# Attention and FFN block on one core: all eight row tiles of a sample in four pairs, and the work around them moved

## The chip, the cores and the metric

The kernel runs on one core of a Trainium2 chip. The time is the device time of one execution in microseconds (us). A core has five engines with queues of their own, and each queue is worked off in order: TensorE (PE in the profile; its weight loads are PEld), VectorE (DVE), ScalarE (ACT), GpSimd (POOL), and SyncE (SP), which issues most of the DMAs.

## The reference

For each of 8 samples `x` has 1024 rows and 256 columns. What is computed, cut to what matters:

```
mod = (silu(c) @ wmod).reshape(8, 6, 1, 256)          # sa, ca, ga, sb, cb, gb; |ga|, |gb| at least 0.25
h = layernorm(x) * (1 + ca) + sa
scores = (h * w_lhs) @ (h * w_rhs).T                  # 1024 x 1024 for each sample
x = x + ga * (softmax(scores) @ h)
h = layernorm(x) * (1 + cb) + sb
x = x + gb * (relu(h @ W1 + b1) @ W2 + b2)            # 256 -> 1024 -> 256
```

All in float32.

## The kernel before, in words

**Tiles.** A sample `b` has eight row tiles `i` of 128 rows. The main loop runs over samples and, in each, over eight steps, one for each tile. Step `i` issues the scores of tile `i + 2` (`direct`), which are copied from PSUM to SBUF by ScalarE (L419). Scores are symmetric (both sides are the same rows, weighted by w_lhs times w_rhs), so only the upper part is computed; the rest comes by a transpose on VectorE (`mirror`, L435) and five DMAs through DRAM (`move`, four writes and one read). VectorE takes the row maximum (L463), TensorE turns it into a row (`max_turn`, L468), VectorE subtracts it (`subtract`, L475), ScalarE takes the exponent (L484). The result is `pT`, the transposed weights of tile `i`: eight blocks of 128x128.

**Product with the values.** `xg` holds the values, eight blocks of 128 rows with 256 columns and a column of ones, whose product is the softmax's sum. A single tile takes eight products 257 columns wide (`product`, L501, tile `po`), a division and a residual addition on VectorE (`product_out`, L513, L515), and the statistics for the next layernorm (L241, L242). A pair of tiles (`i`, `i + 1`) is seen as a 2x2 block product and takes seven half-size products in place of eight: four products of half the rows and 128 or 129 columns are one of the seven. `pair_begin` does two of the seven (L549, tile `pp`), ScalarE copies one of them to `W` (L555), VectorE adds (`pair_begin_sum`, L561). `pair_end` does the other five (L593, tiles `pq` and `pr`), and `pair_out` adds up, divides and adds the residual on VectorE (L608 to L621). The five need sums of the two tiles' weights: `s1` (L565), and three that overwrite parts of `pT` (L575 to L577), all on POOL (`left_sum`, `left_sums`). They also need sums of the values, `tsum`, once for each sample, on POOL too (`right_sums`, L534).

**FFN.** The FFN of the rows of the sample before (its first four tiles in steps 0 to 3, its last four in steps 4 to 7) runs in between. The hidden layer is made in four chunks `c`, two in each of the steps 0 and 1 (4 and 5): `pair_products` (L726; `pa`, `pb`, `pc`), a copy `kept` of `pa` by ScalarE (L747), sums on VectorE (L762 to L771), one more product into `pa` (in `pair_last`, it waits for `kept`), its sum on VectorE (L779), a sum on POOL (L780), the relu on ScalarE (L789, L790), and four sums on POOL (`pair_turn`, L799 to L802, tile `ft`) for the second layer. The second layer is `y_first` in steps 2 and 6 and `y_second` in steps 3 and 7 (L806; `ya` to `yd`), with sums on VectorE (L828 to L830, L848 to L851). Then `y_gate` (ScalarE, L857), `y_turn` (transposes on VectorE, L867, and DMAs) and `y_add` (POOL, L880) bring y back to rows, and `y_out` writes them.

**Order.** All is written out by hand: at the end every instruction is pinned to the order in which it was issued on its engine. `spare` takes one operation from a queue of POOL operations that have no fixed place (`later`). PSUM tiles `pa`, `pb`, `pc`, `pp`, `po`, `pq`, `pr`, `ya` to `yd` share four buffers, so that a product also waits for the reader of an older tile. `Y` has one buffer.

Before the change the tiles of a sample are taken as: 0 alone, 1 and 2, 3 and 4, 5 alone, 6 and 7. In step 0 and 5 stands `product`; pair 1 begins in step 1 and ends in step 2; pair 3 begins in step 3 and ends in step 4; pair 6 begins in step 6 and ends in step 7. The part that decides on it, in the loop's step:

```
if i in (0, 5):
    product(b, i)
    product_out(b, i)
elif i == 1:
    pair_begin(b, i)
    pair_begin_sum(b, i)
elif i == 3:
    left_sums(b, i)
elif i in (2, 4) or i == NT - 1 and ahead:
    pair_end(b, i - 1)
    pair_out(b, i - 1)
```

The first sample (b = 0) has a loop body of its own, with single products only; the change doesn't touch it. After the last sample its FFN follows alone.

Of the kernel before, what the change touches and what calls it, by code (L numbers as in the profile page):

```python
# [11 lines left out]
F32 = mybir.dt.float32  # L12
AF = mybir.ActivationFunctionType
ALU = mybir.AluOpType
# [10 lines left out]
def adaln_block_kernel(  # L25
# [534 lines left out]
        rows = slice(P, P + XS)  # L560
        nc.vector.tensor_tensor(W[:, 0, rows], pp[:, XS : 2 * XS], W[:, 1, rows], ALU.add)  # L561

    def left_sum(b, i):
        s1 = two_t["s1"] = work.tile([P, TH, P], F32, tag="s1", name=f"s1_{b}_{i}", bufs=1)
        nc.gpsimd.tensor_tensor(s1, *halves(pT_t[b, i + 1]), ALU.add)  # L565

    def left_sums(b, i):


        if "s1" not in two_t:  # L570
            left_sum(b, i)
        (a11, a12), (a21, a22) = halves(pT_t[b, i]), halves(pT_t[b, i + 1])
        s1 = two_t["s1"]
        add = nc.gpsimd.tensor_tensor
        add(a21, a11, a21, ALU.subtract)  # L575
        add(a11, s1, a11, ALU.subtract)
        add(a12, a12, a11, ALU.subtract)  # L577
# [66 lines left out]
    def ffn_rstd(b, g):  # L644
        mv = mvb_t.pop((b, g))
        ffn["r", g] = mv, rstd_of(mv, "rb", f"rb_{b}_{g}")
# [206 lines left out]
    def y_gate(b):  # L853

        Y = ffn["Y"]
        for h in range(2):
            nc.scalar.activation(  # L857
                Y[:, h], Y[:, h], AF.Identity,
                scale=gcol[:, 0, h, b : b + 1], bias=gcol[:, 1, h, b : b + 1],
            )  # L860

    def y_turn(b, g, hurry=False):

        Y = ffn["Y"]
        T = two.tile([P, NV, NT * V], F32, tag="T", name=f"T_y{b}_{g}", bufs=3)
        for h in range(2):
            nc.vector.transpose(  # L867
                T.rearrange("p a (t h u) -> p a t h u", h=2, u=V)[:, :, :, h, :],
                Y[:, h].rearrange("p (t a v) -> p a t v", a=NV, v=V),
            )  # L870
        Y = Y.rearrange("p h r -> p (h r)").rearrange("p (b m) -> p b m", b=NV)
        move(Y, T, NT * V, f"y{b}_{g}", hurry)
        ffn["rows", b, g] = Y.rearrange("p b (t h u) -> p t h b u", h=2, u=V)
# [276 lines left out]
    for b in range(B):  # L1150
        for i in range(NT):
# [63 lines left out]
            if first:  # L1215

                ub, ug = (b - 1, 0) if i >= TH else (b - 2, 1)
                back = i % TH == 0 and ub >= 0
                pair_products(fb, fg, c, turn_max)
                if i == 0:  # L1220
                    ffn_rstd(b - 1, 1)
                if i == 4:
                    y_gate(fb)
                    if b + 1 < B:
                        prepare_rstd(b + 1, 1)
                if i == TH + 1:
                    pair_relu(c - 1)
                pair_sums(fb, fg, c)
                if (b, i) == (1, 0):
                    subtract(*late)  # L1230
                if i == 4:
                    y_turn(fb, 0)
                if ahead:
                    mirror(*ahead)
                pair_last(fb, fg, c)
                if i == 0 and back:
                    for q in range(2):
                        y_add(ub, ug, q)
                if i == TH + 1:
                    pair_turn(c - 1)  # L1240
                if late and i != 4 and (b, i) != (1, 0):
                    subtract(*late)
                pair_products(fb, fg, c + 1, (lambda: max_turn(*extra)) if extra else None)
                if (b, i) == (1, 0):
                    exponent(*late)
                    late = None
                if (b, i) == (B - 1, 5):
                    ffn_rstd(b, 0)
                if i == 5:
                    exponent(*late)  # L1250
                    if b + 1 < B:
                        prepare_turn_apart(b + 1, 1, 1)
                        prepare_turn_apart(b + 1, 1, 0)
                if i == 1:
                    exponent(*late)
                    left_sum(b, i)
                elif i == 4 and b + 1 < B:
                    prepare_norm(b + 1, 1)
                    x_plus(b + 1, 1)
                pair_relu(c)  # L1260
                sides_too = i == 4 and b + 1 < B
                if sides_too:
                    prepare_turn_apart(b + 1, 0, 1)
                if late and i == 0:
                    exponent(*late)
                if sides_too:
                    prepare_turn_apart(b + 1, 0, 0)
                middle(b, i)
                pair_sums(fb, fg, c + 1)
                pair_last(fb, fg, c + 1)  # L1270
                if i == 4:
                    if b + 1 < B:
                        prepare_blocks(b + 1, 1)
                        xg_times(b + 1, 1)
                    weights(*late)
                if ahead and ahead != extra:
                    row_max(*ahead)
                pair_turn(c)
                if i == 0:
                    pair_relu(c + 1)  # L1280
                    pair_turn(c + 1)
                if i == 4:
                    for q in range(2):
                        y_add(ub, ug, q)
                if c > 0:
                    pair_relu(c + 1)
                    pair_turn(c + 1)
            else:
                half = i % TH - 2
                if i == NT - 2:  # L1290
                    for q in (1, 3):
                        if (b, q) in two_t:
                            pair_stats(b, q)
                if i == 2:
                    left_sums(b, 1)
                elif i == 3:
                    pair_begin(b, i, turn_max)
                elif i == 6:
                    pair_begin(b, i, lambda: (max_turn(*late), weights(*late)))
                elif not ahead:  # L1300

                    pair_end(b, i - 1)
                    pair_out(b, i - 1)
                    pair_stats(b, i - 1)
                if half:
                    y_second(fb, fg, turn_max if i == NT - 1 else None)
                else:
                    y_first(fb, fg, turn_max if i == 2 else None)
                if ahead:
                    mirror(*ahead)  # L1310
                if i == 2 and b + 1 < B:
                    prepare_rstd(b + 1, 0)
                elif i == 6 and b + 1 < B:
                    ffn_rstd(b, 0)
                elif i == NT - 1 and b == B - 1:
                    ffn_rstd(b, 1)
                if i in (3, 6):
                    pair_begin_sum(b, i)
                if i == 2:
                    weights(*late)  # L1320
                elif i == 6:
                    left_sums(b, i)
                spare()
                early(b, i)
                if late and half:
                    weights(*late)
                middle(b, i)
                if i == 2 and b + 1 < B:
                    load_x(b + 1, 1)
                spare()  # L1330
                if ahead:
                    row_max(*ahead)
                if half:
                    y_second_sums(fb)
                    if i == NT - 1:
                        y_gate(fb)
                    elif b + 1 < B:
                        prepare_stats(b + 1, 1)
                else:
                    y_first_sums()  # L1340
                spare()
            if extra:
                subtract(*extra)
            if i == NT - 1 and 0 < b < B - 1:
                y_turn(fb, fg, True)
            turns(b, i)
            norms(b, i)
            if extra:
# [1 line left out]
            if not first:  # L1350
                for _ in range(4 if half else 1):
                    spare()
            if i in (0, 5):
                product(b, i)
                product_out(b, i)
            elif i == 1:
                pair_begin(b, i)
                pair_begin_sum(b, i)
            elif i == 3:
                left_sums(b, i)  # L1360
            elif i in (2, 4) or i == NT - 1 and ahead:
                pair_end(b, i - 1)
                pair_out(b, i - 1)
                if i == NT - 1:
                    assert not queue
                    right_sums(b + 1, range(4))
                if i == NT - 1 or b == B - 1:
                    pair_stats(b, i - 1)
            late = ahead if ahead != extra else None
            if first and back:  # L1370
                y_out(ub, ug)
            if i == 0 and b + 1 < B:
                load_rows(b + 1)
# [78 lines left out]
```

## Time and profile before

| | |
|---|---|
| median of 3 runs | 756.9 us (756.22 to 757.13) |
| the profiled execution | 756.93 us, span 755.1 us |
| granted TensorE clock | 1.000 |
| busy: TensorE, VectorE, POOL, ScalarE | 749.1, 574.9, 570.9, 374.9 us |
| from one sample's scores of tile 2 to the next one's (b = 4 to 5) | 90.43 us (343.70 to 434.13) |

Times in the profile's rows are microseconds from the start of the span. A row of the timeline gives start, length, engine, line, operation, the tile written and those read, the shape, and how many were merged; in square brackets the engine's idle time before it and what ended it. A float32 product shows as two instructions, so that a count of x8 is four products. Products overlap in their pipeline: what one costs is read from the starts of two that follow each other. In the windows view each engine has its busy time and count of instructions.

### The profile page before, as it was taken

How to read it: one execution, taken by the hardware profiler on the slowest of the kernel's cores; microseconds unless marked ns; L12 is line 12 of the kernel's file. 1: busy time of each engine (PE TensorE's matmuls, PEld its weight loads, DVE VectorE, ACT ScalarE, POOL GpSimd, SP SyncE). 2: the span in 40 equal slices, each digit the busy share in tenths (PEclk: the TensorE clock that was granted, in tenths of full speed). 3: DMA queues.
4: the chain of work that ended last, by engine and by line, in shares of the span. 5: the costliest groups of instructions: out<-in, count | busy, mean ns of one | idle time of the engine just before them, and what ended most of it. 6: DMA issues, size and time to landing. Idle time of an engine off the chain costs nothing.

```text
span 755.1 us, 11883 instructions
## 1 busy us (share of the span) xinstructions
PE 749.1 (99%) x3876; PEld 623.4 (83%) x3876; DVE 574.9 (76%) x1259; ACT 374.9 (50%) x688; POOL 570.9 (76%) x658
## 2 busy tenths in 40 slices
PE   8999999999999999999999999999999999999998
PEld 4686889788897888888888878988889788888887
DVE  7787879778796879968878688876889777685632
ACT  4554646635375454745546444563546535252521
POOL 3762796878968798788877699777996888669741
PEclk9999999999999999999999999999999999999999
DMA  9033442455443453445534555245553354133220
GB/s 308 16 112 98 131 133 74 135 178 152 127 120 123 153 153 110 147 118 158 164 99 119 153 154 161 74 127 172 155 152 85 119 166 133 50 91 126 84 85 28
DMA packets 106213, 95.21 MB, mean 126 GB/s; under 512 B 29700, under 2 KB 98848, under 8 KB 106152
## 3 DMA queue, kind: packets, MB, share of 16 engines
q1 hardware_dynamic: 98408, 85.81, 38.6%
q10 hardware_dynamic: 7744, 8.65, 3.7%
q8 instruction: 30, 0.49, 0.3%
q14 instruction: 31, 0.25, 0.1%
HBM read 50.62 MB, written 43.81 MB: 125 GB/s over the span
## 4 chain that ended last, share of the span: by engine, by line
PE 96%; DMA 1%; DVE 1%; ACT 1%; issue 0%
PE psc L412 16%; PE pa L726 11%; PE po L501 10%; PE pr L593 7%; PE pb L726 7%; PE pc L726 7%; PE yc L806 6%; PE ya L806 6%; PE yb L806 6%; PE pq L593 5%; PE pp L549 5%; PE py L916 4%; PE yd L806 3%; DMA wm<-in_L_wmod_dram 1%; PE pm L468 1%; PE pmr L194 0%
## 5 line engine op out<-in xcount | busy, mean ns | idle before, releaser
L412 PE MATMUL psc<-rT,lT 128*128 128x512 f32 (+3 forms) x384 | 134.8, 487 | 0.0
L780 POOL TENSOR_TENSOR f<-f,kept 128x512 f32<-128x512 f32 x64 | 81.5, 1274 | 42.8 <-DVE f L779 20.1
L419 ACT COPY sc<-psc 128x512 f32<-128x512 f32 (+3 forms) x96 | 44.7, 476 | 119.9 <-PE psc L412 113.0
L484 ACT ACTIVATE pT<-pT 128x1024 f32<-128x1024 f32 x64 | 67.6, 1056 | 70.6 <-DVE pT L475 70.5
L475 DVE TENSOR_TENSOR pT<-sc,pm 128x1024 f32<-128x1024 f32 x64 | 77.3, 1208 | 29.3 <-PE pm L468 13.7
L412 PEld LDWEIGHTS psc<-rT,lT 128*128 128x128 f32 x384 | 66.4, 191 | 37.2 <-issue 25.6
L501 PE MATMUL po<-xg,pT 128*128 128x257 f32 x352 | 80.6, 380 | 0.0
L463 DVE TENSOR_REDUCE m<-sc 128x1 f32<-128x1024 f32 x64 | 77.4, 1209 | 2.2 <-ACT sc L419 1.8
L501 PEld LDWEIGHTS po<-xg,pT 128*128 128x128 f32 x352 | 66.2, 190 | 10.0 <-issue 0.7
L747 ACT COPY kept<-pa 128x512 f32<-128x512 f32 x64 | 37.4, 584 | 69.3 <-PE pa L726 69.1
L726 PE MATMUL pb<-hs,w1s 128*128 128x256 f32 x256 | 65.9, 380 | 0.1
L726 PE MATMUL pc<-hT,w 128*128 128x256 f32 x256 | 65.7, 379 | 0.0
L880 POOL TENSOR_TENSOR x<-x,Y 128x512 f32<-128x512 f32 x28 | 35.1, 1276 | 29.3 <-DMA Y<-D_y 29.3
L789 ACT ACTIVATE f<-f 128x512 f32<-128x512 f32 x64 | 39.8, 622 | 34.7 <-POOL f L780 34.7
L642 POOL TENSOR_TENSOR x<-x,rows 128x256 f32<-128x256 f32 x64 | 44.8, 732 | 13.8 <-ACT rows L1022 10.6
L726 PEld LDWEIGHTS pb<-hs,w1s 128*128 128x128 f32 x256 | 48.5, 190 | 7.3 <-DVE f L765 0.8
L726 PEld LDWEIGHTS pc<-hT,w 128*128 128x128 f32 x256 | 48.6, 190 | 6.7
L806 PE MATMUL yc<-f,w2s 128*128 128x256 f32 x224 | 51.3, 379 | 0.0
L435 DVE STREAM_TRANSPOSE Tm<-sc 128x896 f32<-128x896 f32 (+6 forms) x49 | 34.3, 701 | 20.3 <-ACT sc L419 19.6
L806 PEld LDWEIGHTS yc<-f,w2s 128*128 128x128 f32 x224 | 41.5, 190 | 8.1 <-issue 2.9
L549 PEld LDWEIGHTS pp<-xg,pT 128*128 128x128 f32 x336 | 41.9, 192 | 5.1 <-DVE st_b L241 1.4
L799 POOL TENSOR_TENSOR ft<-f 128x256 f32<-128x256 f32 x56 | 40.8, 729 | 6.8 <-ACT f L790 6.8
(166 smaller groups left out, 1821.1 us busy)
## 6 DMA issues: line engine op xcount, KB each, us to landing
D_f<-T_f SPq DMA_DIRECT2D x60, 128.0 KB, 2.5
X_f<-D_f SPq DMA_DIRECT2D x15, 512.0 KB, 3.7
D_a<-T_a SPq DMA_DIRECT2D x56, 128.0 KB, 2.8
D_y<-T_y SPq DMA_DIRECT2D x56, 128.0 KB, 2.9
Y<-D_y SPq DMA_DIRECT2D x14, 512.0 KB, 3.4
out_dram<-x SPq DMA_DIRECT2D x14, 512.0 KB, 4.4
X_a<-D_a SPq DMA_DIRECT2D x13, 512.0 KB, 3.4
x<-in_L_attn_x_dram ACTq DMA_DIRECT2D x12, 512.0 KB, 3.4
```

Of the source, the lines that this page charges most:

```text
L412: nc.tensor.matmul(psc[:, : hi - lo], lhsT=lT_t[b, i // TH][:, k, ts(i % TH, P)], rhs=rT_t[b, n][:, k, lo - n * HALF : HALF], start=(k == ...
L419: nc.scalar.copy(score_row(b, i)[:, lo // V : hi // V, :], psc[:, : hi - lo].rearrange("p (n v) -> p n v", v=V),)
L463: nc.vector.tensor_reduce(m, score_row(b, i), AX.XY, ALU.max)
L475: nc.vector.tensor_tensor(pT.rearrange("p j (a v) -> p j a v", v=V), score_columns(b, i), pm[:, :P].rearrange("p (j a v) -> p j a v", j=1, ...
L484: nc.scalar.activation(pT_t[b, i], pT_t[b, i], AF.Exp)
L501: nc.tensor.matmul(po[:, : D + 1], lhsT=pT[:, t, :], rhs=xg_t[b][:, t, 0 : D + 1], start=(t == 0), stop=(t == NT - 1),)
L549: nc.tensor.matmul(out, lhsT=lhs[:, t, :], rhs=xg_t[b][:, h * TH + t, P : P + XS], start=(t == 0), stop=(t == TH - 1),)
L593: nc.tensor.matmul(out, lhsT=lhs[:, t, :], rhs=rhs[:, t, :], start=(t == 0), stop=(t == TH - 1),)
L642: queue.append(lambda: nc.gpsimd.tensor_tensor(out, in0, row, op))
L726: nc.tensor.matmul(out, lhsT=lhsT, rhs=rhs, start=True, stop=True)
L780: nc.gpsimd.tensor_tensor(f[:, c::NH, hi], f[:, c::NH, hi], kept[:, None, hi].to_broadcast([P, 2, H2]), ALU.add,)
L806: nc.tensor.matmul(out, lhsT=lhs(c), rhs=rhs(c), start=(c == 0), stop=(c == NH - 1))
```

## The change

Four pairs in every sample from b = 1 on: 0 and 1, 2 and 3, 4 and 5, 6 and 7. A pair begins at the end of the steps 0 and 4 and near the start of the steps 2 and 6. It ends at the end of the steps 1 and 5, and for pair 2 and pair 6 at the start of the steps 3 and 7, ahead of `y_second`. In step 7 the additions `pair_out` of pair 6 stand ahead of the sums of `y_second`, and the right side's sums for the next sample are issued there, behind all that is left in POOL's queue. Gate and transposes of y (`y_gate`, `y_turn`) move from step 7 (and 4) into the steps 0 and 4, behind the sums of the first chunk; y's additions and the output's DMA move from the steps 0 and 4 to the steps 1 and 5. The left sums of pairs 0 and 4 stand in the steps 1 and 5, between the two chunks of these steps, and the sums `ft` of chunk 1 move behind them. Statistics of the finished tiles move to steps 3, 6 and 7 (for the last sample one of them to step 5).

The diff:

```diff
--- before.py
+++ after.py
@@ -560,17 +560,12 @@
         rows = slice(P, P + XS)
         nc.vector.tensor_tensor(W[:, 0, rows], pp[:, XS : 2 * XS], W[:, 1, rows], ALU.add)
 
-    def left_sum(b, i):
+    def left_sums(b, i):
+
+
         s1 = two_t["s1"] = work.tile([P, TH, P], F32, tag="s1", name=f"s1_{b}_{i}", bufs=1)
         nc.gpsimd.tensor_tensor(s1, *halves(pT_t[b, i + 1]), ALU.add)
-
-    def left_sums(b, i):
-
-
-        if "s1" not in two_t:
-            left_sum(b, i)
         (a11, a12), (a21, a22) = halves(pT_t[b, i]), halves(pT_t[b, i + 1])
-        s1 = two_t["s1"]
         add = nc.gpsimd.tensor_tensor
         add(a21, a11, a21, ALU.subtract)
         add(a11, s1, a11, ALU.subtract)
@@ -1216,11 +1211,13 @@
 
                 ub, ug = (b - 1, 0) if i >= TH else (b - 2, 1)
                 back = i % TH == 0 and ub >= 0
+                returned = i % TH == 1 and ub >= 0
                 pair_products(fb, fg, c, turn_max)
                 if i == 0:
                     ffn_rstd(b - 1, 1)
+                if back:
+                    y_gate(ub)
                 if i == 4:
-                    y_gate(fb)
                     if b + 1 < B:
                         prepare_rstd(b + 1, 1)
                 if i == TH + 1:
@@ -1228,16 +1225,17 @@
                 pair_sums(fb, fg, c)
                 if (b, i) == (1, 0):
                     subtract(*late)
-                if i == 4:
-                    y_turn(fb, 0)
+                if back:
+                    y_turn(ub, ug)
                 if ahead:
                     mirror(*ahead)
+                if i % TH == 1:
+                    left_sums(b, i - 1)
                 pair_last(fb, fg, c)
-                if i == 0 and back:
-                    for q in range(2):
-                        y_add(ub, ug, q)
-                if i == TH + 1:
+                if i % TH == 1:
                     pair_turn(c - 1)
+                if (b, i) == (B - 1, 5):
+                    pair_stats(b, 2)
                 if late and i != 4 and (b, i) != (1, 0):
                     subtract(*late)
                 pair_products(fb, fg, c + 1, (lambda: max_turn(*extra)) if extra else None)
@@ -1253,7 +1251,6 @@
                         prepare_turn_apart(b + 1, 1, 0)
                 if i == 1:
                     exponent(*late)
-                    left_sum(b, i)
                 elif i == 4 and b + 1 < B:
                     prepare_norm(b + 1, 1)
                     x_plus(b + 1, 1)
@@ -1275,35 +1272,34 @@
                     weights(*late)
                 if ahead and ahead != extra:
                     row_max(*ahead)
+                if returned:
+                    for q in range(2):
+                        y_add(ub, ug, q)
                 pair_turn(c)
                 if i == 0:
                     pair_relu(c + 1)
-                    pair_turn(c + 1)
-                if i == 4:
-                    for q in range(2):
-                        y_add(ub, ug, q)
                 if c > 0:
                     pair_relu(c + 1)
                     pair_turn(c + 1)
             else:
                 half = i % TH - 2
-                if i == NT - 2:
-                    for q in (1, 3):
-                        if (b, q) in two_t:
-                            pair_stats(b, q)
+                if i == NT - 2 and b < B - 1:
+                    pair_stats(b, 2)
                 if i == 2:
-                    left_sums(b, 1)
+                    pair_begin(b, i)
                 elif i == 3:
-                    pair_begin(b, i, turn_max)
+                    turn_max()
                 elif i == 6:
                     pair_begin(b, i, lambda: (max_turn(*late), weights(*late)))
-                elif not ahead:
-
+                else:
+                    turn_max()
                     pair_end(b, i - 1)
-                    pair_out(b, i - 1)
-                    pair_stats(b, i - 1)
+                    if not ahead:
+
+                        pair_out(b, i - 1)
+                        pair_stats(b, i - 1)
                 if half:
-                    y_second(fb, fg, turn_max if i == NT - 1 else None)
+                    y_second(fb, fg)
                 else:
                     y_first(fb, fg, turn_max if i == 2 else None)
                 if ahead:
@@ -1314,11 +1310,10 @@
                     ffn_rstd(b, 0)
                 elif i == NT - 1 and b == B - 1:
                     ffn_rstd(b, 1)
-                if i in (3, 6):
+                if not half:
                     pair_begin_sum(b, i)
-                if i == 2:
-                    weights(*late)
-                elif i == 6:
+                    if i == 2:
+                        weights(*late)
                     left_sums(b, i)
                 spare()
                 early(b, i)
@@ -1331,18 +1326,26 @@
                 if ahead:
                     row_max(*ahead)
                 if half:
+                    if i == NT - 1 and ahead:
+                        pair_out(b, i - 1)
                     y_second_sums(fb)
-                    if i == NT - 1:
+                    if i == NT - 1 and b == B - 1:
                         y_gate(fb)
-                    elif b + 1 < B:
-                        prepare_stats(b + 1, 1)
+                    elif i == 3:
+                        pair_stats(b, 0)
+                        if b + 1 < B:
+                            prepare_stats(b + 1, 1)
                 else:
                     y_first_sums()
+                    if i == NT - 2:
+                        pair_stats(b, 4)
                 spare()
             if extra:
                 subtract(*extra)
             if i == NT - 1 and 0 < b < B - 1:
-                y_turn(fb, fg, True)
+                while queue:
+                    spare()
+                right_sums(b + 1, range(4))
             turns(b, i)
             norms(b, i)
             if extra:
@@ -1350,24 +1353,16 @@
             if not first:
                 for _ in range(4 if half else 1):
                     spare()
-            if i in (0, 5):
-                product(b, i)
-                product_out(b, i)
-            elif i == 1:
+            if i in (0, 4):
                 pair_begin(b, i)
                 pair_begin_sum(b, i)
-            elif i == 3:
-                left_sums(b, i)
-            elif i in (2, 4) or i == NT - 1 and ahead:
+            elif i in (1, 3, 5):
                 pair_end(b, i - 1)
                 pair_out(b, i - 1)
-                if i == NT - 1:
-                    assert not queue
-                    right_sums(b + 1, range(4))
-                if i == NT - 1 or b == B - 1:
-                    pair_stats(b, i - 1)
+            elif i == NT - 1 and ahead:
+                pair_stats(b, i - 1)
             late = ahead if ahead != extra else None
-            if first and back:
+            if first and returned:
                 y_out(ub, ug)
             if i == 0 and b + 1 < B:
                 load_rows(b + 1)
```

## The prediction

> **What bounds the kernel now.** I read the page first, then the list of waits, then the timelines of one middle sample (b=4, which starts at 343.70) on each engine.
>
> ```profile
> span 755.1 us, 11883 instructions
> PE 749.1 (99%) x3876; PEld 623.4 (83%) x3876; DVE 574.9 (76%) x1259; ACT 374.9 (50%) x688; POOL 570.9 (76%) x658
> ...
> PE 96%; DMA 1%; DVE 1%; ACT 1%; issue 0%
> ```
>
> TensorE is the bound, and not only as an average: in the list of waits its longest wait inside a sample is 0.3 us. So a microsecond less on TensorE counts in full, and so does each wait that it meets. The timelines show how little early the others are. TensorE in the second half of the sample (tiles 4 to 7; it starts with the scores of tile 6 at 387.58):
>
> ```profile
> 394.17 0.59 PE L726 MATMUL pa<-hT,w1s 128*128 128x256 f32 x2
> 394.60 1.05 PE L593 MATMUL pr<-tsum,s 128*128 128x128 f32 x8
> ...
> 398.17 1.06 PE L593 MATMUL pr<-xg,pT 128*128 128x128 f32 x8
> 399.06 0.61 PE L412 MATMUL psc<-rT,lT 128*128 128x128 f32 x4
> 399.51 0.60 PE L726 MATMUL pa<-hT,w 128*128 128x256 f32 x2
> ...
> 402.21 0.60 PE L726 MATMUL pa<-hT,w1s 128*128 128x256 f32 x2
> ```
>
> The last product of FFN chunk 2 (402.21) overwrites half of `pa` and waits for ScalarE's copy `kept` of it. ScalarE:
>
> ```profile
> 393.98 2.08 ACT L281 ACTIVATE xg<-x,rs,ra 128x256 f32<-128x256 f32 x4 [0.76 <-DVE rs L277]
> 395.97 0.61 ACT L789 ACTIVATE f<-f 128x512 f32<-128x512 f32 x1
> ...
> 397.01 1.50 ACT L342 ACTIVATE rT<-X_a,sides 128x512 f32<-128x512 f32 x2
> 398.42 1.51 ACT L342 ACTIVATE lT<-X_a,sides 128x512 f32<-128x512 f32 x2
> 399.83 1.04 ACT L484 ACTIVATE pT<-pT 128x1024 f32<-128x1024 f32 x1
> 400.77 0.24 ACT L419 COPY sc<-psc 128x128 f32<-128x128 f32 x1
> 400.92 0.58 ACT L747 COPY kept<-pa 128x512 f32<-128x512 f32 x1
> ```
>
> It works without a gap from 393.98 to 401.50, and is 0.7 us early. POOL in the first half (from 343.70):
>
> ```profile
> 352.51 2.52 POOL L880 TENSOR_TENSOR x<-x,Y 128x512 f32<-128x512 f32 x2
> 354.98 1.27 POOL L780 TENSOR_TENSOR f<-f,kept 128x512 f32<-128x512 f32 x1
> ...
> 371.27 0.73 POOL L800 TENSOR_TENSOR ft<-ft,f 128x256 f32<-128x256 f32 x1
> ```
>
> Its `ft` of chunk 3 ends at 372.00; TensorE's third `ya` group (371.29, four steps of 0.43) reads it at 372.59: 0.6 us early. The windows view (busy us of TensorE, its weight loads, VectorE, ScalarE, POOL, with instructions in brackets) says the same of the stage: POOL is busy 41.3 of the first half's 43.9 us, though 76% over the whole.
>
> ```profile
> 343.70:387.60 43.90, 43.90 (x231) 36.92 (x230) 34.95 (x78) 19.75 (x38) 41.28 (x49) 1.00 0.53 153
> 387.60:434.10 46.50, 46.50 (x253) 39.52 (x252) 36.42 (x80) 27.96 (x49) 32.53 (x37) 1.00 0.42 123
> ```
>
> **The change part by part, TensorE.** Removed per sample: two single products, 3.46 us each (352.44 to 355.90). Added: one pair, 1.79 (L549, 364.22 to 366.01) + 4.46 (L593, 394.60 to 399.06) = 6.25. Gain 0.67 us, over seven samples 4.7. But the order changes too, and this is where I expect the loss. In the times below t counts from each half's first score product; where TensorE "comes" is the sum of its pieces without waits.
>
> **Second half: ScalarE comes too late.** The 4.46 us of the pair's end stood between chunks 1 and 2; now its beginning (1.79) stands there. TensorE comes to chunk 2's last product at 7.02 (394.60) + 1.79 + 0.45 + 2.70 (399.51 to 402.21) = 11.96, before 14.63. ScalarE's row up to `kept` starts from `rs` on VectorE, which follows chunk 0's products, all before the edit's place; it ends at 13.92 as before, plus one `W` copy queued ahead (L555, 0.26): 14.15. Wait 2.2 to 2.4, I take 2.3. Behind the waiting product all of chunk 3 is queued, so nothing overtakes. It holds for samples 1 to 6. The last sample has no `xg` and no `rT`/`lT` there (5 us less).
>
> **First half: y's rows and the left sums.** Gate (L857, two, 1.5 us) and transposes (L867, 1.3 us) of y move from the step before to between chunk 0's sums and its last sum L779 on VectorE. That sum ends at 8.7 instead of 7.43 (350.75 + 0.38), and chunk 1's at 12.15 instead of 10.84. `pp` of pair 0 takes the buffer that L779 frees: wait 0.2. ScalarE's relu waits for POOL's L780 behind L779, so its row (relu 1.2, exponent 1.0, `X_f` 2.1, relu 1.2, `W`, scores) brings `kept` of chunk 2 at 16.7; TensorE comes at 8.74+1.79+2.17+2.70 = 15.4, before 17.07. Wait 1.3 to 1.5.
>
> Longer still is POOL. All of pair 0's left sums, 4 x 1.27 = 5.1 (rows L565, L575 to L577), stand ahead of chunk 2 and 3, where before only one (1.27) did; the additions of y's rows (2.5) no longer fill POOL's idle time at 352.5 but stand behind chunk 3. From L780 of chunk 1 at 12.25 it runs without pause: 1.25, turn of four 3.0, sums 5.1, 1.25, 3.0, 1.25, rows 2.5, turn 3.0, two more 1.55: `ft` of chunk 3 at 34.3. TensorE comes to it at 8.74+1.79+2.17+5.72+0.43+4.46+1.72+1.79+3.45+0.11+1.30 = 31.7 and loads weights 0.2 earlier (after 10.5: scores from 355.90 to 358.07, chunks 2 and 3 from 358.07 to 363.79 and their last product, the pair's end, scores from 366.01 to 367.73, a pair's beginning, two y groups, the max's turn, three steps of four). The wait is 2.85 and contains the 1.4 for `kept`. Sample 1 has no earlier y here: there only `kept` counts (88.35-72.13 = 16.22, + 0.25 against 15.2: 1.25).
>
> **Start of the first half.** The last pair's end stands ahead of y's second products, so `hT` on VectorE now follows y's last sum, 0.2 us after TensorE left `yd`, instead of 0.9 us before it. 0.54 + `hT` + three `hs` (2.1, L714 to L716) = third `hs` at 3.2 to 3.9; it is wanted at 3.25. `hT` takes 0.51 with POOL idle (433.19) and 1.21 where a POOL sum had begun first (647.85); POOL's right sums end just there. Wait 0 to 0.65, I take 0.3.
> [...]
>
> **Costed at nothing.** The right sums (5.1) moved up: POOL ends them about when `hs` is wanted, else the wait above grows. VectorE's larger pair end (L608 to L621, 2.5, and L561, 0.28, for two single ends of 0.65) and the moved statistics: cover is VectorE's idle time, 9 to 10 us in each half; in the second half they stand where statistics stood before `u` at 390.44. Uncovered, the pair end's difference of 1.5 us would count per sample. SP: y's four writes now precede four mirror writes. The second half already has that order: there the mirror's read is issued 4.7 us after its transpose (393.57 to 398.28). 8.35 + 4.7 + 3.4 (landing of the other reads on the page) = 16.5, and VectorE reads it at 19.5. The output's DMA waits for y's additions (29.8), and the load that waits for it on ScalarE's queue comes at 36; the output lands 4.4 us after issue. Were it late, ScalarE's queue would stand still with `hT` behind it.
>
> **Last sample.** First half: pair 2 begins there, pair 0 ends there, so 2 x 1.79 + 4.46 and another 4.46 (12.5) for 3.46 + 2 x 1.79 + 4.46 (11.5), plus 2.85 + 0.3: +4.15. Second half: before it took 694.70-658.95 = 35.75, with 1.0 of waits. Now POOL has 5.1 of sums before chunk 2, `ft` of chunk 3 comes at 30.5 where TensorE wants it at 27.3, then the last pair's sums follow directly (four of 1.3, to 37.1), and its last product starts at 37.2 and ends at 38.1: +2.35.
>
> **Sum.** Samples 2 to 6: 5 x (-0.67 + 2.85 + 2.3 + 0.3 = +4.8) = 23.9. Sample 1: -0.67 + 1.25 + 2.3 = 2.9. Last: 6.5. Together +33.3. The profiled execution took 756.93 (span 755.1 and 1.8 around it), 0.03 over the median 756.9. 756.9 + 33 = 790; I say 789.
>
> **The rivals.**
> - Only ScalarE's order hurts, POOL keeps up in the first half: 1.4 instead of 2.85 there, six times: 789 - 9 = 780. For it: POOL idles 16.6 us per sample (windows above, 2.6 + 14.0). Against: nearly all of that lies in the second half.
> - POOL slows too, since more of it runs beside VectorE: its `ft` operations step by 0.69 to 0.81; all at 0.81 is 1.5 us more in each first half and 0.5 in each second: 789 + 12 = 801.
> - Other side: the covers hold and only the gain is left, 756.9 - 4.7 = 752. It decides at one place: `kept` of chunk 2 must be ready at 11.75 and 15.2; ScalarE would have to be 2.4 us faster in the second half. Against: its row there has no gap. That the edit leaves the program unchanged is excluded by the order of instructions.
>
> **How the numbers follow.** The stated sum 0.62, POOL keeping up 0.16, POOL slower 0.13, gain alone 0.09. What can be told from no change is 0.2% (1.5 us). Faster 0.08 and same 0.01 both come from the last case, slower 0.91. The range goes beyond the cases of 780 and 801: below, half the second half's wait (6 x 1.15 = 7) and the wait for `hs` (6 x 0.3 = 2) could also be absent, 771; above, `hs` could be late by its upper bound (6 x 0.35 = 2 more), 803. So 771 to 803.
>
> **What would show it.** TensorE idle or with stretched products at L747's `kept` in both halves and at the third `ya` group; waits "PE or PEld pa <- ACT kept" near 2 us, 6 times, and "ya <- POOL ft" near 1.4 us, 6 times; a period of about 95.2 us per sample. I am wrong if `kept` of chunk 2 precedes its product, or if POOL reaches chunk 3 before TensorE.

## The result

The changed kernel takes 794.39 us (median of 4 runs, 791.1 to 795.38) against 757.01 us before on the same chip: 1.0488 times as long, 95% interval 1.0456 to 1.0521. Forecast were 789 and the range 771 to 803. The page of the changed kernel, its busy times, the clock by slices and the chain:

```profile
span 793.4 us, 12327 instructions
PE 759.5 (96%) x4044; PEld 627.1 (79%) x4044; DVE 592.1 (75%) x1294; ACT 374.2 (47%) x695; POOL 606.9 (76%) x686
...
PE 53%; POOL 15%; DVE 12%; ACT 8%; DMA 5%; issue 4%; SPq 1%; DVEq 0%; POOLq 0%; ACTq 0%
```

TensorE fell from 99% to 96% of the span, and its part of the chain from 96% to 53%: the chain now runs through the engines that TensorE waits for. Which these are, the list of TensorE's waits says (us in total, times, longest):

```profile
PE pa L721 <- ACT kept L742: 16.5, 13, 1.7
PE ya L801 <- POOL ft L795: 4.0, 6, 0.8
PE ya L801 <- ACT Y L813: 2.6, 1, 2.6
PE pq L588 <- DVE f L760: 2.4, 5, 1.2
PE pb L721 <- POOL hs L711: 1.9, 6, 0.7
PE pw L143 <- DVE early_a L131: 1.5, 1, 1.5
PE pm L468 <- DVE m L463: 1.0, 6, 0.2
```

Before, only `pw` and, with 0.3 us, the `ACT Y` line were among these. This view counts idle time alone; part of a wait shows as a stretched product (0.70 at 421.30 below, 0.60 for the same product at 402.21 in the kernel before). Below, a wait is therefore the step from the product before to the late one, less the usual step of the same two. The product behind a late one starts another 0.1 late (421.84 after 421.30 below: 0.54 in place of 0.43); this is not in the waits and counted apart. (Line numbers are 5 lower than before's; experiments have their own.)

The second half of sample 4, whose scores of tile 6 start at 407.11, on TensorE:

```profile
418.09 1.03 PE L721 MATMUL pc<-hT,w 128*128 128x256 f32 x4
419.27 0.32 PE L468 MATMUL pm<-ident,m 128*128 128x128 f32 x1 [0.16 <-DVE m L463]
421.30 0.70 PE L721 MATMUL pa<-hT,w1s 128*128 128x256 f32 x2 [1.70 <-ACT kept L742]
421.84 0.59 PE L721 MATMUL pa<-hT,w 128*128 128x256 f32 x2
```

and on ScalarE:

```profile
413.58 2.08 ACT L281 ACTIVATE xg<-x,rs,ra 128x256 f32<-128x256 f32 x4 [0.82 <-DVE rs L277]
...
419.42 1.04 ACT L484 ACTIVATE pT<-pT 128x1024 f32<-128x1024 f32 x1
420.37 0.24 ACT L555 COPY W<-pp 128x129 f32<-128x129 f32 x1
420.51 0.25 ACT L419 COPY sc<-psc 128x128 f32<-128x128 f32 x1
420.67 0.58 ACT L742 COPY kept<-pa 128x512 f32<-128x512 f32 x1
```

ScalarE's row has no gap, as before, and `kept` ends at 421.25, which is t = 14.14 (forecast 14.15). TensorE waits 1.92 for it and 0.33 for the row maximum just ahead of it: 2.25 in each of the six halves (forecast 2.3).

In the first half (359.58 for sample 4) TensorE waits 1.08 for `kept`, 0.3 to 0.55 at the start of the pair's end, and 0.7 to 0.9 at the third `ya` group. TensorE and POOL there:

```profile
391.83 1.46 PE L801 MATMUL ya<-ft,w2s 128*128 128x256 f32 x6
393.80 0.70 PE L801 MATMUL ya<-ft,w2s 128*128 128x256 f32 x2 [0.50 <-POOL ft L795]
```

```profile
386.71 2.57 POOL L875 TENSOR_TENSOR x<-x,Y 128x512 f32<-128x512 f32 x2
...
392.21 0.73 POOL L794 TENSOR_TENSOR ft<-f 128x256 f32<-128x256 f32 x1
393.02 0.72 POOL L795 TENSOR_TENSOR ft<-ft,f 128x256 f32<-128x256 f32 x1
```

`ft` of chunk 3 ends at 393.74, t = 34.16 (forecast 34.3); y's additions stand ahead of it.

**One thing the forecast did not have: the clock.** The granted clock of the profiled execution is 0.993. Windows of 3.41 us, as long as the clock stays low from 133.75 on (busy us of TensorE first; the clock is the third column from the end):

```profile
130.34:133.75 3.41, 1.54 (x7) 1.19 (x7) 1.60 (x5) 3.22 (x7) 2.73 (x4) 1.00 0.63 157
133.75:137.16 3.41, 3.41 (x10) 2.70 (x9) 2.92 (x6) 1.64 (x2) 3.25 (x4) 0.50 0.48 169
225.92:229.33 3.41, 1.76 (x8) 1.07 (x6) 1.84 (x3) 3.41 (x7) 2.69 (x4) 1.00 0.29 48
229.33:232.74 3.41, 3.18 (x15) 2.82 (x16) 3.17 (x7) 1.81 (x4) 3.25 (x3) 1.00 0.85 283
321.53:324.94 3.41, 1.54 (x8) 0.87 (x6) 1.64 (x4) 3.41 (x8) 2.72 (x4) 0.99 0.32 50
...
720.84:724.25 3.41, 1.43 (x7) 1.28 (x8) 0.70 (x2) 1.49 (x3) 3.24 (x5) 1.00 0.71 179
724.25:727.66 3.41, 3.41 (x10) 2.69 (x9) 0.42 (x1) 0.81 (x1) 3.33 (x4) 0.50 1.07 378
```

After three of the seven waits of 2.2 us or more (samples 1 and 3, and the last one's second half) the clock is at a half for 3.4 us; after the one of sample 2, in the third and fourth row, it is not. That costs half of 3.4 each, 5.1 together. The profiled execution is the longest of the four: their clocks were 1.000, 0.996, 0.993 and 0.993, the times 791.1, 793.8, 795.0 and 795.4. The one that kept its clock took 791.1, against the 790 that the forecast had worked out.

Where the time came from, by sample, from the starts of the scores of tile 2 (before to after, the lowered clock's 1.7 taken out where it falls):

| | forecast | measured |
|---|---|---|
| sample 1 | +2.9 | +3.1 |
| samples 2 to 6, mean | +4.8 | +4.8 |
| last sample, first half | +4.15 | +4.14 |
| last sample, second half, to the products behind its last pair | +2.35 | +1.7 |
| the FFN behind it (a wait for `hs`) | 0 | +0.5 |
| sum | +33.3 | +33.4 |
| lowered clock | not foreseen | +5.1 |

With the start of the program (-0.2) this is the 38.3 us between the two spans.

### The profile page after: what moved, and what is told of

Read it like the earlier page. It is cut to its first block, busy times and chain, and to the rows that moved or that the text cites. A ratio compares the mean times of both kernels' runs of the same rounds, so it can differ in the third digit from the quotient of the medians.

```text
span 793.4 us, 12327 instructions
## 1 busy us (share of the span) xinstructions
PE 759.5 (96%) x4044; PEld 627.1 (79%) x4044; DVE 592.1 (75%) x1294; ACT 374.2 (47%) x695; POOL 606.9 (76%) x686
## 4 chain that ended last, share of the span: by engine, by line
PE 53%; POOL 15%; DVE 12%; ACT 8%; DMA 5%; issue 4%; SPq 1%; DVEq 0%; POOLq 0%; ACTq 0%
PE psc L412 10%; PE pr L588 6%; PE yc L801 5%; PE pq L588 5%; PE yb L801 4%; PE pa L721 4%; PE po L501 4%; PE ya L801 3%; POOL f L775 3%; PE pb L721 3%; PE yd L801 3%; DMA sc<-D_m 2%; DMA D_m<-Tm 2%; POOL x L875 2%; DVE T_y L862 2%
## 5 line engine op out<-in xcount | busy, mean ns | idle before, releaser
L475 DVE TENSOR_TENSOR pT<-sc,pm 128x1024 f32<-128x1024 f32 x64 | 77.1, 1205 | 33.4 <-PE pm L468 16.1
L721 PE MATMUL pb<-hs,w1s 128*128 128x256 f32 x256 | 67.6, 387 | 1.9 <-POOL hs L711 1.9
L588 PE MATMUL pq<-tsum,pT 128*128 128x128 f32 (+1 forms) x448 | 60.0, 277 | 2.8 <-DVE f L760 2.4
L549 PEld LDWEIGHTS pp<-xg,pT 128*128 128x128 f32 x448 | 54.4, 192 | 7.7 <-issue 6.2
L588 PEld LDWEIGHTS pq<-tsum,pT 128*128 128x128 f32 x448 | 54.5, 192 | 4.3 <-DVE f L760 4.3
L549 PE MATMUL pp<-xg,pT 128*128 128x129 f32 x448 | 55.6, 275 | 0.0
L721 PE MATMUL pa<-hT,w1s 128*128 128x256 f32 x128 | 39.7, 394 | 16.5 <-ACT kept L742 16.5
L757 DVE SCALAR_TENSOR_TENSOR u<-pb,cols,kept 128x256 f32<-128x256 f32 x64 | 30.6, 478 | 30.5 <-PE pb L721 21.1
```

The lines of the kernel that those rows point to most:

```text
L475: nc.vector.tensor_tensor(pT.rearrange("p j (a v) -> p j a v", v=V), score_columns(b, i), pm[:, :P].rearrange("p (j a v) -> p j a v", j=1, ...
L549: nc.tensor.matmul(out, lhsT=lhs[:, t, :], rhs=xg_t[b][:, h * TH + t, P : P + XS], start=(t == 0), stop=(t == TH - 1),)
L588: nc.tensor.matmul(out, lhsT=lhs[:, t, :], rhs=rhs[:, t, :], start=(t == 0), stop=(t == TH - 1),)
L721: nc.tensor.matmul(out, lhsT=lhsT, rhs=rhs, start=True, stop=True)
```

## The experiments

My theory: the order is what costs. TensorE comes earlier, ScalarE's and POOL's rows are full where it comes, and each wait hides the next. The rival that fits the result as well: POOL has 36 us more work (570.9 to 606.9) and VectorE 17, they slow each other, and no order helps. Half lengths below are from tile 2's scores to tile 6's (first half, samples 2 to 6) and on to the next sample's (second half, samples 1 to 6, those with lowered clock left out); each kernel's times are beside runs of the kernel before of 757.0 to 757.7 median.

**rT and lT behind chunk 3's `kept`** (second half).

```diff
-                sides_too = i == 4 and b + 1 < B
-                if sides_too:
-                    prepare_turn_apart(b + 1, 0, 1)
 ...
-                if sides_too:
-                    prepare_turn_apart(b + 1, 0, 0)
 # step 5, after pair_products(fb, fg, c + 1), if there is a next sample:
+                        prepare_turn_apart(b + 1, 0, 1)
+                        prepare_turn_apart(b + 1, 0, 0)
                     exponent(*late)
```

> The changed kernel with one move in the second half of samples 1 to 6: ScalarE's four copies rT/lT for the next sample's first four tiles stand behind chunk 3's kept, no longer ahead of chunk 2's. Theory (the loss is the order: TensorE comes 2.7 us earlier to a copy that ScalarE can't have done): the wait of 2.25 us for kept of chunk 2 goes. Late next is rT of the next sample's last four tiles, whose read lands at 428.75 (b=4) with its two copies done at 429.56 and 430.27, where the scores then want them at 428.8 and 429.2: a new wait of 1.1. Gain 6 x (2.25 - 1.1) = 6.9, and some 2.5 us of lowered clock that followed the waits: 794.4 - 9 = 785 (782 to 788). Rival (the loss is that POOL and VectorE do more work and slow each other, wherever a copy stands): 794 (792 to 796).

Measured: 788.09 (788.07 to 788.35), a hair above the range. The second half went from 47.23 to 45.97. The mechanism was half right. The wait shrank by 1.26, not by all of it, and no wait for `rT` came. What is left is 1.1, as much as was forecast for `rT`, but that is luck: it is 0.33 for the row maximum, 0.67 for `kept` and 0.1 behind it. ScalarE in this kernel:

```profile
411.19 0.62 ACT L785 ACTIVATE f<-f 128x512 f32<-128x512 f32 x1
413.24 1.06 ACT L484 ACTIVATE pT<-pT 128x1024 f32<-128x1024 f32 x1 [1.44 <-DVE pT L475]
...
414.51 0.60 ACT L742 COPY kept<-pa 128x512 f32<-128x512 f32 x1
```

Next in the way was the exponent of tile 5, which waits for VectorE, with `kept` behind it. And TensorE, earlier now, waits longer at the next place: for `hs` at the start of the first half 0.93 in place of 0.44 on average.

**SP's order too.** The same, with the writes of the next sample's tiles ahead of two reads (the two calls are shown; `move` takes their last argument).

```diff
-                    mirror(*ahead)
+                    mirror(*ahead, not (i == 4 and b + 1 < B))    # its read is held back
 ...
-                        prepare_blocks(b + 1, 1)
+                        prepare_blocks(b + 1, 1, None, "last")    # writes, held reads, own read
```

> The run above, and on SP's queue the four writes for the next sample's last four tiles go ahead of the two reads that they stood behind (mirror's and y's), the read of the tiles itself behind them. Theory: rT comes some 2 to 3 us earlier, its wait of 1.1 goes; late next is POOL's ft of chunk 3, at about 437.8 where TensorE then wants it at 437.0: 0.8. 794.4 - 6 x (2.25 - 0.8) - 2.5 = 783 (780 to 786). Rival (POOL and VectorE): 794, as in the run above.

Measured: 793.98 (792.64 to 796.02): missed, all of the gain is gone. VectorE and TensorE:

```profile
422.19 1.22 DVE L478 TENSOR_TENSOR pT<-sc,pm 128x1024 f32<-128x1024 f32 x1 [2.13 <-DMA sc<-D_m]
```

```profile
424.38 1.16 PE L591 MATMUL pq<-tsum,pT 128*128 128x128 f32 x8 [1.74 <-DVE f L763]
```

The read of tile 6's mirror now lands too late for the subtraction; chunk 3's sums stand behind it on VectorE, and `pq` needs the buffer that they free. I had not asked who needed the reads that I held back.

**Relu of chunk 1 behind `kept`** (first half).

```diff
-                if i == TH + 1:
+                if i % TH == 1:
                     pair_relu(c - 1)
 ...
-                if i == 0:
-                    pair_relu(c + 1)
```

> The changed kernel with the relu of chunk 1 (1.2 us on ScalarE) behind kept of chunk 2 in the first half; nothing else. Theory (POOL's row bounds the first half, and the wait for kept is contained in it): kept's wait of 1.08 goes, the one at the third ya group grows by as much. Only sample 1, which has no y to add there, gains 0.95: 793.4 (792 to 795). Rival (the two waits add up): 6 x 1.05 less, 788 (787 to 789).

Measured: 793.67 (792.3 to 795.26), as the theory has it. Its waits:

```profile
PE pa L721 <- ACT kept L742: 10.2, 6, 1.7
PE ya L801 <- POOL ft L795: 7.2, 6, 1.5
PE pq L588 <- DVE f L760: 5.5, 7, 1.4
```

All seven of `kept`'s waits in first halves are gone (13 times to 6), and `ya` and `pq` grew by 6.3 us together. Sample 1's first half fell from 46.42 to 45.37, the others did not (47.96 to 48.76, mean 48.14; 48.05 without the move). TensorE comes no earlier to the third `ya` group (34.66 to 35.45 after the half's start; 34.21 to 35.23 without the move), so the wait for `kept` lay inside POOL's. Half of it only moved to `pq`, which stands behind VectorE: in sample 4 the subtraction there waits 0.59 for the read of a mirror (DMA `sc` <- `D_m`), with chunk 3's sums behind it.

**ft split.** Two of the four sums of each chunk go behind chunk 3's.

```diff
         add(ft[:, 1, c], ft[:, 0, c], f[:, c, lo], ALU.add)
+    def pair_turn_rest(c):          # called for all four chunks behind the last pair_turn
 ...
         add(ft[:, 2, c], ft[:, 1, c], f[:, c + NH, lo], ALU.subtract)
         add(f[:, c, hi], f[:, c, hi], f[:, c, lo], ALU.subtract)
```

> The changed kernel with POOL's four sums ft of a chunk split: the two that the first y products read stay, the two that only the second y products read stand behind chunk 3's, for all four chunks. The same sums, in another order. Theory: ft of chunk 3 comes some 4 us earlier, the wait at the third ya group goes (0.85 in samples 2 to 6, 0.95 and 2.77 in the last one's halves), kept's waits stay: 794.4 - 8 = 786.5, another 1.7 less if the last half's lowered clock goes with its wait (784 to 788). Rival (POOL's amount of work is what counts): 794 (792 to 796).

Measured: 793.21 (792.73 to 793.38): the number is the rival's. The wait that I aimed at did go, but others took its place:

```profile
PE pb L721 <- POOL hs L711: 4.3, 7, 0.7
PE pa L721 <- POOL hs L709: 1.3, 2, 1.1
PE ya L805 <- ACT Y L817: 1.3, 1, 1.3
PE pr L588 <- POOL s L567: 1.0, 1, 1.0
```

The line "`ya` <- POOL `ft`" is absent. In its place TensorE waits at the start of the next first half for `hs`, which stands on POOL behind the right sums. These end 1.2 to 3.5 us after the half's start (from 0.4 before it to 1.4 after it in the changed kernel). After this run the two theories stood open: one order after another, or POOL's amount.

**Tiles 4 and 5 alone again** (first half and pair 6-7 as changed).

```diff
-            if i in (0, 4):
+            if i in (4, 5):
+                product(b, i)
+                product_out(b, i)
+            elif i == 0:
                 pair_begin(b, i)
                 pair_begin_sum(b, i)
-            elif i in (1, 3, 5):
+            elif i in (1, 3):
 ...
```

(The left sums of pair 4 and one statistic in step 6 go with the pair.)

> The changed kernel with its first half as it is (pairs 0-1 and 2-3, y's move) and tiles 4 and 5 alone again in the second half, pair 6-7 as it is: as many pairs, and as much POOL work, as the kernel before. Theory (the order): a single product (3.46) stands where the pair's beginning (1.79) stood ahead of chunk 2, so the waits there (2.25 with the row maximum's 0.33) shrink to about 0.6, and the last half's first wait (1.37) goes; the first half keeps its 3.2 us. 794.4 - 6 x (2.25 - 0.6 - 0.67) - 1.4 and 2 to 4 us of lowered clock: 785 (781 to 788). Rival (POOL's amount of work, 36 us more than before, is what costs): back to 757 to 762.

Measured: 778.41 (778.25 to 779.57), clock 1.000. Its busy times:

```profile
PE 756.4 (97%) x3876; PEld 622.5 (80%) x3876; DVE 575.3 (74%) x1259; ACT 372.9 (48%) x688; POOL 571.2 (74%) x658
```

POOL and VectorE do the work of before (570.9 and 574.9), and the kernel is still 21 us slower: the amount is not the cause of these 21. It was faster than I forecast, since four terms were counted low or not at all: the second half is 46.06 (47.23 in the changed kernel, for six halves 7.0 us), the last half 2.6 us shorter, the wait for `hs` is gone in samples 2 to 6 (2.2), and with no wait over 1.1 us the clock stays up (5.1). Together 16.9 of the 17.1 us between the spans.

**The cost of a late `kept`, in the kernel before.** More copies ahead of it.

```diff
+        if c == 2 and g == 1 and b < B - 2:
+            for _ in range(5):          # or range(1)
+                nc.scalar.copy(kept, pa)
         nc.scalar.copy(kept, pa)
```

> The kernel before with five more copies of the same tile (0.5 us each from start to start) ahead of ScalarE's kept of chunk 2 in the second half of samples 1 to 6; nothing else. Theory (0.7 us early there, and every further us is paid by TensorE): 6 x (2.5 - 0.7) = 10.8, 768 (766 to 770), up to 772 if the clock is lowered after some of these waits as it is in the changed kernel. Rival (later slack hides a late copy): 757 to 760.

> The same with one more copy (0.5 us). Theory (0.7 us early): no change, 757 (756 to 758). Rival (ScalarE's row is already on the path there): 6 x 0.5 = 3 us more, 760.

Measured: one copy 757.91 (ratio 1.0001, 0.9992 to 1.0010), no change; five copies 776.99 (776.82 to 778.17). The forecast for five was too low by the size of a copy and the clock:

```profile
411.97 3.04 ACT L749 COPY kept<-pa 128x512 f32<-128x512 f32 x5
415.04 0.58 ACT L750 COPY kept<-pa 128x512 f32<-128x512 f32 x1
```

```profile
413.15 0.27 PE L468 MATMUL pm<-ident,m 128*128 128x128 f32 x1
415.68 0.70 PE L726 MATMUL pa<-hT,w1s 128*128 128x256 f32 x2 [2.25 <-ACT kept L750]
```

Five copies take 3.07 (0.61 each, not 0.5), and TensorE waits 2.42: the cover was 0.65, where 0.7 was read from the trace. Six such waits are 14.5 us; the clock was lowered after two of them (3.4), and for 3.4 us at the start of the program too, which was 2.0 us longer (the scores of tile 2 in sample 1 start at 74.10 in place of 72.13). Together 19.9 of the 20.2 us between the two spans.

**All orders together.** First five moves, then eight, then two more for what was left.

```diff
 # step 5 (ScalarE): tile 5's exponent behind chunk 2's kept
+                if i == TH + 1:
+                    exponent(*held)
 # step 7 (VectorE, POOL): hT ahead of y's last sums, hs ahead of the right sums
                         pair_out(b, i - 1)
+                        while queue:
+                            spare()
+                        turns(b, i)
+                        right_sums(b + 1, range(4))
                     y_second_sums(fb)
 ...
 # steps 1 and 5 (VectorE): subtraction behind chunk 3's sums
                 pair_sums(fb, fg, c + 1)
+                if i == 1:
+                    subtract(*late)
                 pair_last(fb, fg, c + 1)
+                if i == 5 and not plain:
+                    subtract(*late)
```

These are three of the moves, as they stand in the last kernel. In the first of the kernels three of the four right sums still stood ahead of `hs`.

> The changed kernel with five moves and no work added or left out: rT/lT behind chunk 3's kept and tile 5's exponent behind chunk 2's (second half, ScalarE); relu of chunk 1 behind chunk 2's kept (first half, ScalarE); ft split as in r4 (POOL); hT ahead of y's last sums on VectorE, and hs ahead of the last of the four right sums on POOL. Theory: each wait by itself gains little, since the next one takes it (r1, r4), but together they go and the 0.67 us per sample of TensorE's gain shows: 756.9 - 4.7 = 752, plus what I left (row maximum 0.33 x 6, pq 0.4 x 6, last sample 4): 760 (755 to 768). Rival (POOL's amount): not under 780.

> The five moves, with all four right sums behind hs (in the run with five moves hs waited for three of them, 1.7 us at the start of each first half), and: tiles 4 and 5 of the last sample alone (as in h1, where its last half had 4 us less); rs for the next sample's norm ahead of y's transposes on VectorE; in steps 1 and 5 the subtraction behind chunk 3's sums, and tile 6's maximum turned inside chunk 3. Theory: what is left of waits is about 0.5 per sample, so TensorE's gain shows: 756.9 - 4.7 + 6 x 0.5 = 755 (751 to 762). Rival (POOL's row has no room for the fourth pair): not under 768.

> The run above without its last two moves (subtraction and tile 6's maximum stay where the changed kernel has them). Theory: the row maximum's 0.33 and the first half's pq (0.4 to 1.3) stay: 6 x 0.8 more than the run above, 760 (756 to 766). Rival (POOL's row): not under 768.

> The eight moves, and for the two waits that were left: SP issues the next sample's last four tiles' writes ahead of the read of tile 6's mirror (r2 did this where the subtraction that needs that read stood earlier; it now has some 4 us more), and the last sample's second half keeps ft unsplit and its old order of subtractions. Theory: rT's wait (0.5 to 1.3, six times) and the last half's 3.5 us go: 764.3 - 6 - 3.5 = 755 (752 to 760), under the kernel before by about 0.3%. Rival (SP's queue only hands the wait to tile 6's mirror again, as in r2): 764 or more.

| | time | first half | second half | largest waits left |
|---|---|---|---|---|
| before | 757.0 | 43.88 | 46.55 | |
| changed | 794.39 | 47.5 to 48.5 | 47.23 | above |
| five moves | 779.67 (779.33 to 780.35) | 47.3 to 48.4 | 45.4 to 46.2 | `hs` 1.7, `pq` 0.3 to 1.3, last half 4.9 |
| eight, without the last two | 768.06 (767.66 to 769.8) | 45.5 to 46.0 | 45.5 to 46.7 | `rT` 0.1 to 1.5, `pq` 0.4 to 0.8, last half 3.6 |
| eight | 764.29 (763.42 to 765.5) | 45.05 | 45.7 to 46.3 | `rT` 0.5 to 1.3, last half 3.4 |
| and two more | 755.37 (754.87 to 756.08) | 45.05 | 44.88 | last half 2.2 |

The five moves, the eight and the eight without two miss what I had forecast for them (760, 755 and 760), each since I had not seen the next wait: three right sums ahead of `hs`, then `rT`, and in the last half the moved sums ahead of the pair's `s1` (2.6). By the bounds that were set for the rival, the five moves (779.67, bound 780) and the eight without two (768.06, bound 768) decide nothing; the eight (764.29, bound 768) and the last kernel (755.37, bound 764) speak against it. The last kernel gives what I forecast. Its ratio to the kernel before (8 runs against 12) is 0.9972 (0.9962 to 0.9983): faster than both kernels. Its page and the longest of its waits inside a sample:

```profile
span 753.5 us, 12246 instructions
PE 745.6 (99%) x4020; PEld 623.4 (83%) x4020; DVE 579.2 (77%) x1289; ACT 375.9 (50%) x694; POOL 600.9 (80%) x682
...
PE pr L596 <- POOL s L575: 1.1, 1, 1.1
```

POOL has 30 us more work than before, in a shorter span; so the rival fails on this side too. A sample takes 45.05 + 44.88 = 89.93 in place of 90.43. (In its last sample tiles 4 and 5 are alone and the split is left out.)

## Why the prediction was right, and where it was off

- **TensorE's gain, 0.67 per sample.** Right in size: where the waits are gone, a sample is 0.50 shorter (0.1 of the rest is one late product in its first half). In the changed kernel it lies under the waits: in samples 2 to 6 they add up to 5.5 per sample, and the sample is 4.8 longer.
- **Second half, ScalarE too late: 2.3.** Measured 2.25. The place, the engine and the moment were right, but the row maximum's 0.33 ahead of it was not named, and the first move showed what stands next behind the copies `rT`/`lT`: an exponent that waits for VectorE. Of the 2.25, `kept` itself takes 1.92, where 2.2 to 2.4 was forecast for it alone.
- **First half, 2.85 in all, 1.4 of it for `kept`.** Measured 1.08 for `kept`, some 0.4 at `pq`, some 0.8 at `ya`: 2.3, with 0.44 for `hs` 2.75, and with 0.1 behind each of the four 3.1 (forecast 3.15 with `hs`). The place that bounds the half, POOL's `ft`, was right; that the sum comes out so well is partly luck, since `ya` alone is 0.6 below its forecast 1.4, and `pq` and the 0.1 behind each wait were not in it. That `kept`'s wait lies inside POOL's was shown by moving the relu. The stop at `pq` was not foreseen: it waits for a buffer that chunk 3's sums free.
- **Start of the first half, 0 to 0.65, taken 0.3.** Measured 0 to 0.90, mean 0.44. The right sums, costed at nothing with the warning "else the wait above grows", were the next bound: with `rT` and `lT` moved the wait grew to 0.93 on average, with `ft` split to 1.25, with the five moves to 1.6. At this place VectorE's `hT` took 0.54 to 1.09 in this kernel, and up to 1.62 in the first experiment, 1.08 more than with POOL idle (0.54, at 455.91 in the changed kernel):

```profile
638.11 1.62 DVE L700 TENSOR_SCALAR hT<-X_f,modT 128x512 f32<-128x512 f32 x1
```

```profile
638.18 1.27 POOL L534 TENSOR_TENSOR tsum<-tsum,xg 128x512 f32<-128x512 f32 x1
```

A whole POOL sum lies inside it, and `hT` ends 0.28 after that sum. The rows that the forecast went by had only 0.7 more than undisturbed (1.21 for 0.51).
- **Last sample +6.5.** Measured 5.9 without the clock, and 0.5 more in the FFN behind it. In the second half one wait was named, for `ft`, and what followed it; there were two others, 1.37 at `pq` and 2.77 at `ya` (the one for `Y` in the list). `ft` of chunk 3 ends 30.4 after the half's start, forecast 30.5, but `ya` waits for ScalarE's copy `Y` (722.39): it stands behind the exponent of tile 7, which waits for a subtraction on VectorE behind the pair's additions (717.02 to 720.04). So this half's size is near for another reason than the forecast's.
- **Covers.** y's writes, its read and the output's DMA stayed hidden, as argued: "POOL `x` <- DMA `Y`" fell from 29.3 us to 6.6, and no wait of TensorE in the list above is for a load.
- **The rivals.** POOL doesn't keep up, so 780 fails; its operations are hardly slower either (from `ft` to `ft` 0.762 on average, 0.758 before), so 801 fails; the covers don't hold, so 752 fails.
- **What was missing: "756.9 + 33 = 790" had no term for the clock.** Without it the sum was 33.4; the other 5.1 of the profiled execution came from TensorE's clock, which the profile of before shows at 1.000, with no wait of this length inside a sample. For saying 789 where 790 was worked out the forecast gives no reason.

One sentence of the description ahead of the prediction is wrong: pair 2's end stands at the end of step 3, behind `y_second`; only pair 6's stands ahead of it.

## What to carry to other kernels

Where one engine is 99% busy, look at how early each of the others is at the place that the edit moves, not at how busy they are: here covers of 0.6 to 0.7 us decided over a gain of 0.67. A wait that is taken away gains only up to the next one (the first move gained 1.26 of 2.25); so list the next two before choosing an edit, and ask of each transfer or sum that is put back who stands behind it. And a wait of TensorE can cost more than its length: after three of the seven waits of 2.2 us or more in the changed kernel the clock was 0.50 for 3.4 us, 1.7 us each.

## What the runs showed of the hardware

TensorE's clock was lowered to 0.50 for 3.4 us after some waits of 2.2 to 2.8 us (three of seven), and not after others of the same length; the kernel before, given such waits by five copies, showed it too (after two of six), and the kernels without them (tiles 4 and 5 alone; all moves) not or hardly: the clocks of their profiled executions are 1.000 and 0.999.

In the 3.41 us ahead of the three starts (133.75, 324.9, 724.25) TensorE was busy 1.54, 1.54 and 1.43 us. That does not set these waits apart from the others: stretches of the same length around the waits of samples 2 and 4 were busy 1.53 and 1.54, and the clock was 1.00 in them and in the 3.41 us behind them.

```profile
226.40:229.81 3.41, 1.53 (x7) 0.89 (x6) 1.64 (x3) 3.41 (x7) 2.71 (x4) 1.00 0.36 79
229.81:233.22 3.41, 3.41 (x17) 3.00 (x17) 3.34 (x8) 1.80 (x4) 3.17 (x4) 1.00 0.75 248
418.00:421.41 3.41, 1.54 (x8) 0.88 (x7) 1.64 (x4) 3.41 (x8) 2.71 (x4) 1.00 0.27 50
421.41:424.82 3.41, 3.41 (x16) 3.02 (x17) 3.37 (x7) 1.80 (x4) 3.17 (x4) 1.00 0.86 281
```

What decides between these cases stays open.
